# The last layer's loop in a four-layer transformer: another order of work, queries in SBUF, mixing in smaller steps

## The chip, the cores and the metric

The kernel runs on one core of a Trainium2 chip. The metric is the device time of one execution in microseconds. The profile names the engines PE (TensorE, matrix products, with PEld for loading its weights), DVE (VectorE), ACT (ScalarE), POOL (GpSimd) and SP (SyncE, which issues DMAs).

## What is computed

The reference runs four transformer layers on an input of 16×256×128. Each layer has an attention and a second block, each behind a layer norm with a shift and a scale from a small conditioning vector, and each added to the input with a gate. Only the last layer matters here. Its attention runs over the first axis, of length 16, separately for each of the 256 columns, causally, with 16 heads of 8 numbers. Its second block is a channel mixing with the row before:

```
scores = einsum("bhqd,bhkd->bhqk", q, k) / sqrt(8)      # q, k index the axis of 16, b the 256 columns
attn = softmax(where(causal, scores, -inf))
x = x + ga * (attn @ v @ W_out + b_out)
h = layernorm(x) * (1 + cb) + sb
xr, xk = mu * h + (1 - mu) * h_prev                     # h_prev: the column before
x = x + gb * sigmoid(xr @ W_r.T) * (relu(xk @ W_k.T) ** 2 @ W_v.T)
```

## The kernel before

The data x lie in SBUF as 128 channels by 16 units of 256 columns; a unit u is one position of the attention's axis. A query of unit u needs the keys of units 0 to u, so the work of a unit grows with u. Since each column has its own tiny attention, the scores are no matrix product over columns. Instead, for unit u:

- `queries`: PE makes the query, 128×256, in PSUM (tile q in the pool ps_q).
- `scores`: DVE multiplies the query, plus its bias, with the keys of up to 8 units at once (tile qk). Above 8 keys the unit has two parts, c=0 and c=1.
- `heads`: PE sums over the 8 channels of a head (16 small products a part) into the tile S.
- `exps`: DVE takes the maximum (top) and subtracts it (E), ACT takes the exponential.
- `weights`: DVE sums over the keys and inverts (tot), POOL multiplies E by that.
- `spread`: PE spreads the weights back over the channels, half a part at a time, into one of two large PSUM tiles (ps_big).
- `weighted`: DVE multiplies them with the values (tile pv); after the second half POOL adds the keys up in a tree until one or two are left.
- `projected`: PE multiplies what is left with the output weights (tile A). `added`: ACT scales it (tile t) and POOL adds it to x.

The loop of `layer3` (L2301) runs over u from 0 to 18. In iteration u it does scores and heads of unit u, exps and weights of w=u-1, spread and weighted of z=u-2, projected and added of a=u-3. Beside that run generators, the sides: `keys3` makes keys and values of two later units, `mixing3` does the second block of two finished units (of one unit for the last two). Each `tick()` lets every side do its next step. Both begin with the normalisation `normed3`: mean by a product on PE, difference on DVE (ln_xc), square on ACT (ln_sq), mean on PE, logarithm and exponential on ACT, product on POOL. `mixing3` goes on with `shifted` (ACT, tile h3f), two mixed products of four matmuls on PE, a sigmoid made from absolute value, relu, exponential and logarithm on ACT (tiles h and r, a sum on POOL), relu and square for the other (kr), a product with W_v on PE, the gating on DVE (r), the sum on POOL and the output DMA on SP.

Inside the loop `strict` and `strict_all` are set, and `keep_in_program_order` then fixes the order on each engine as the program issues it. An engine that waits therefore holds up all that the program issued after it on that engine. PSUM has eight banks: four in ps_big, one for ps_q, three for `bank()`, which serves S, A and all steps of the sides. Most operations are recorded on one line, L225 (the class that keeps the order) or L271 (`mm`), so the profile is read by the names of tiles.

Of the kernel before, what the change touches and what calls it, by code (L numbers as in the profile page):

```python
# [23 lines left out]
P = 128  # L24
# [186 lines left out]
def bc(ap, shape):  # L211
    return ap.to_broadcast(shape)
# [20 lines left out]
class _Kernel:  # L233
# [1982 lines left out]
        m = self.mods[3]  # L2216
        self.act.activation(dst, src, AF.Identity, bias=m[:, 3 * half, b : b + 1], scale=m[:, 3 * half + 1, b : b + 1])

    def normed3(self, src, out):

        n = src.shape[-1]
        ps = self.bank()[:, :n]
        self.mm(ps, self.c("mean"), src)
        yield
        xc = self.ln.tile([P, BLK], F32, tag="ln_xc", name="ln_xc")[:, :n]
        self.dve.tensor_sub(xc, src, ps)
        sq = self.ln.tile([P, BLK], F32, tag="ln_sq", name="ln_sq")[:, :n]
        self.act.activation(sq, xc, AF.Square)
        yield
        ps = self.bank()[:, :n]  # L2230
        self.mm(ps, self.c("mean"), sq)
        yield
        self.act.activation(sq, ps, AF.Ln, bias=self.eps5)
        self.act.activation(sq, sq, AF.Exp, scale=-0.5)
        self.gps.tensor_mul(xc, xc, sq)
        out.append(xc)
        yield

    def keys3(self, blk):

        out = []
        yield from self.normed3(self.x[:, blk * BLK : (blk + 1) * BLK], out)
        h = self.h3[blk] = self.l3.tile([P, BLK], F32, tag="h3", name="h3", bufs=3)
        for i in range(2):
            self.shifted(h[:, i * T : (i + 1) * T], out[0][:, i * T : (i + 1) * T], 2 * blk + i, 0)
        yield
        for n, (dst, k) in enumerate(((self.k3, "a3_bk"), (self.v3, "a3_bv"))):
            ps = self.bank()
            self.mm(ps, self.w3[:, (n + 1) * P : (n + 2) * P], h)
            yield  # L2250
            self.act.activation(dst[:, 2 * blk : 2 * blk + 2, :].rearrange("p b t -> p (b t)"), ps, AF.Identity, bias=self.v(k))

    def mixing3(self, b0, nb):

        two, W = self.two3, nb * T
        x = self.x[:, b0 * T : (b0 + nb) * T]
        if nb == 2:
            yield
            yield
        out = []  # L2260
        yield from self.normed3(x, out)

        h = two.tile([P, 2, T + 1], F32, tag="h3f", name="h3f")
        self.gps.memset(h[:, :, 0:1], 0.0)
        for i in range(nb):
            self.shifted(h[:, i, 1:], out[0][:, i * T : (i + 1) * T], b0 + i, 1)
        yield

        def mixed(n):
            ps = self.bank()[:, :W]  # L2270
            o = ps.rearrange("p (b t) -> p b t", t=T)
            self.mm(o, self.mix[2 * n], h[:, :nb, 1:], start=True, stop=False)
            self.mm(o, self.mix[2 * n + 1], h[:, :nb, :T], start=False, stop=True)
            return ps

        ps = mixed(0)
        yield

        r = two.tile([P, BLK], F32, tag="r3", name="r3")[:, :W]
        l = self.h1[:, :W]  # L2280
        self.act.activation(l, ps, AF.Abs)
        self.act.activation(r, ps, AF.Relu, scale=-1.0)
        self.act.activation(l, l, AF.Exp, scale=-1.0)
        self.act.activation(l, l, AF.Ln, bias=self.one)
        self.gps.tensor_add(r, r, l)
        ps = mixed(1)
        yield
        k = two.tile([P, BLK], F32, tag="kr3", name="kr3")[:, :W]
        self.act.activation(k, ps, AF.Relu)
        self.act.activation(k, k, AF.Square)  # L2290
        self.act.activation(r, r, AF.Exp, scale=-1.0)
        ps = self.bank()[:, :W]
        self.mm(ps, self.wv3, k)
        yield
        for i in range(nb):
            c = slice(i * T, (i + 1) * T)
            self.dve.scalar_tensor_tensor(r[:, c], ps[:, c], self.mods[3][:, 5, b0 + i : b0 + i + 1], r[:, c], ALU.mult, ALU.mult)
        self.gps.tensor_add(x, x, r)
        self.nc.sync.dma_start(out=self.out[:, b0 * T : (b0 + nb) * T], in_=x)

    def layer3(self):  # L2301
        self.tables()
        m = self.mods[3]
        with ExitStack() as ctx:
            self.ps_big = self.pool("ps_big", 2, PSUM, ctx=ctx)
            self.ps_q = self.pool("ps_q", 1, PSUM, ctx=ctx)
            self.ps_one = self.pool("ps_three", 3, PSUM, ctx=ctx)
            two = self.two3 = self.ln = self.pool("a3_two", 2, ctx=ctx)
            C = 32
            U = [{} for _ in range(B)]  # L2310
            sides = []

            def tick():
                for g in list(sides):
# [7 lines left out]
                return [(0, n)] if n <= 8 else [(0, (n + 1) // 2), ((n + 1) // 2, n)]  # L2322

            def queries(u):
                q = U[u]["q"] = self.ps_q.tile([P, T], F32, tag="q", name="ps_q")
                self.mm(q, self.w3[:, :P], self.h3[u // 2][:, u % 2 * T : (u % 2 + 1) * T])

            def scores(u, c):
                d = U[u]
                k0, k1 = parts(u)[c]  # L2330
                n = k1 - k0
                p = d["p", c] = self.wide.tile([P, 8, T], F32, tag="qT", name="qk")
                self.dve.scalar_tensor_tensor(
                    p[:, :n], bc(d["q"].unsqueeze(1), [P, n, T]), self.v("a3_bq"), self.k3[:, k0:k1, :], ALU.add, ALU.mult
                )

            def heads(u, c):
                d = U[u]
# [39 lines left out]
            def weighted(u, c, half):  # L2378
                d = U[u]
                k0, k1 = parts(u)[c]  # L2380
                n = k1 - k0
                if half == 0:
                    d["w", c] = (self.w if c else self.wide).tile([P, 8, T], F32, tag="wqkv" if c else "kT", name="pv")
                p = d["w", c]
                o = p[:, :n, half * P : (half + 1) * P].rearrange("p k (g c) -> p g k c", c=C)
                v = self.v3[:, k0:k1, half * P : (half + 1) * P].rearrange("p k (g c) -> p g k c", c=C)
                self.dve.tensor_mul(o, d.pop(("X", c, half))[:, :, :n], v)
                if half == 1:

                    add = (self.dve if u == B - 1 and c == 1 else self.gps).tensor_add  # L2390
                    while n > 2:
                        h = n // 2
                        add(p[:, :h], p[:, :h], p[:, n - h : n])
                        n -= h
                    d["n", c] = n
# [6 lines left out]
                    self.mm(d["A"], self.wo3, p, start=k == 0, stop=k == len(P_) - 1)  # L2402

            def added(u):
                t = two.tile([P, T], F32, tag="t3", name="t3")
                self.act.activation(t, U[u]["A"], AF.Identity, bias=self.go3[:, u : u + 1], scale=m[:, 2, u : u + 1])
                xb = self.x[:, u * T : (u + 1) * T]
                self.gps.tensor_add(xb, xb, t)
                U[u] = None
                if u >= B - 2:  # L2410
                    sides.append(self.mixing3(u, 1))
                elif u % 2:
                    sides.append(self.mixing3(u - 1, 2))

            self.strict = self.strict_all = True
# [2 lines left out]
            for u in range(B + 3):  # L2420
                w, z, a = u - 1, u - 2, u - 3
                b = u // 2 + 3
                if u % 2 == 0 and b < NBLK:
                    made[b] = self.keys3(b)
                    sides.append(made[b])
                if u == B + 2:
                    projected(a)
                    added(a)
                    break
                on_u, on_w, on_z, on_a = (0 <= i < B for i in (u, w, z, a))  # L2430
                two_u, two_z = on_u and u >= 8, on_z and z >= 8
                if on_z:
                    spread(z, 0, 0)
                    spread(z, 0, 1)
                if on_w:
                    exps(w)
                if on_u:
                    scores(u, 0)
                tick()
                if on_z:  # L2440
                    weighted(z, 0, 0)
                if two_z:
                    spread(z, 1, 0)
                if on_u:
                    heads(u, 0)
                if on_w:
                    weights(w)
                if on_a:
                    projected(a)
                if on_z:  # L2450
                    weighted(z, 0, 1)
                if two_z:
                    spread(z, 1, 1)
                tick()
                if two_u:
                    scores(u, 1)
                if two_z:
                    weighted(z, 1, 0)
                    tick()
                if two_u:  # L2460
                    heads(u, 1)
                if two_z:
                    weighted(z, 1, 1)
                if on_a:
                    added(a)
                tick()
                if u + 1 < B:
                    g = made.pop((u + 1) // 2, None)
                    if g in sides:
# [1 line left out]
                            pass  # L2471
                        sides.remove(g)
                    queries(u + 1)
                tick()
            while sides:
                tick()
            self.strict = self.strict_all = False
# [29 lines left out]
```

## Time and profile before

| what | value |
|---|---|
| timed runs | 2811.62, 2819.05, 2821.82 us, median 2819.05 |
| profiled execution | 2796.98 us, span from first to last instruction 2795.3 us |
| busy over the span | PE 2533.1 us (91%), DVE 1859.2 (67%), ACT 1588.3 (57%), POOL 1255.8 (45%) |
| mean granted clock of PE | 0.969 |
| the last layer | from 2574 us to the end of the span |

In the views below, a group's row gives line, engine, operation and out<-in with the shapes; a wait's row gives who waited for whom, the total in us, how often, and the longest. "Idle before" names the instruction that ended an engine's wait. The profiled execution is one execution and is 22 us shorter than the median of the timed runs; sums of rows are made against its own time.

### The profile page before, as it was taken

The page shows a single profiled execution, that of the slowest core. Times are in us where ns is not written, and L with a number is a line of the kernel's source. Part 1 is how long each engine was busy: PE and PEld are TensorE (multiplying, and loading weights), DVE is VectorE, ACT ScalarE, POOL GpSimd, SP SyncE. Part 2 cuts the span into 40 slices and gives each one's busy share as a digit, 9 for nine tenths or more (in the row PEclk, how much of TensorE's full clock was granted, in tenths as well). Part 3 has the DMA queues.
Part 4 walks back from the last instruction along what each step waited for, and adds up shares of the span by engine and source line. Part 5 has one row for each costly group of instructions (what it writes and reads, how often), then busy time and mean ns, then how long its engine had stood idle before and what let it go on. Part 6 is the DMA issues. An engine that isn't in the chain of part 4 may idle for free.

```text
span 2795.3 us, 50159 instructions
## 1 busy us (share of the span) xinstructions
PE 2533.1 (91%) x17702; PEld 1674.2 (60%) x17702; DVE 1859.2 (67%) x4448; ACT 1588.3 (57%) x4166; POOL 1255.8 (45%) x1105
## 2 busy tenths in 40 slices
PE   7999999989799999999999888899978998999886
PEld 4566565655588677777767545557745565444443
DVE  6777777787654466666666778783367885654664
ACT  4666666666544555666666366675535655542523
POOL 5776786886413553344434300233566442000555
PEclk9999999999999999999999899998989999999988
DMA  9230000000177300000000122326733331221000
GB/s 334 36 42 1 7 10 1 11 27 5 36 213 216 98 16 1 3 1 1 1 31 5 43 93 78 108 67 192 222 91 107 99 93 48 80 82 58 8 8 16
DMA packets 119434, 181.23 MB, mean 65 GB/s; under 512 B 18112, under 2 KB 81152, under 8 KB 116880
## 3 DMA queue, kind: packets, MB, share of 16 engines
q1 hardware_dynamic: 97504, 148.64, 17.9%
q0 software_dynamic: 8432, 17.31, 2.1%
q10 hardware_dynamic: 13248, 12.06, 1.3%
q8 instruction: 142, 2.33, 0.3%
q14 instruction: 108, 0.88, 0.1%
HBM read 120.51 MB, written 60.58 MB: 65 GB/s over the span
## 4 chain that ended last, share of the span: by engine, by line
PE 51%; DVE 22%; ACT 13%; POOL 5%; issue 5%; DMA 2%; SPq 1%; DVEq 0%; ACTq 0%; POOLq 0%
PE ps_one L271 23%; PE ps_big L271 8%; ACT E L225 7%; PE ps_one L274 6%; PE ps_out L271 5%; PE ps_hid L271 4%; DVE m L225 4%; POOL E L225 3%; PE ps_max L271 3%; DVE PT L225 2%; DVE r_t L225 2%; DVE sm_neg L225 1%; ACT r_sq L225 1%; PE ps_exp L271 1%; SPq L1431 1%
## 5 line engine op out<-in xcount | busy, mean ns | idle before, releaser
L225 POOL TENSOR_TENSOR E<-E,sm_inv 128x1024 f32<-128x1024 f32 (+1 forms) x246 | 412.8, 1688 | 502.6 <-DVE sm_inv L225 464.8
L225 ACT ACTIVATE E<-E,sm_neg 128x256 f32<-128x256 f32 x512 | 252.8, 495 | 198.3 <-DVE sm_neg L1216 198.3
L225 ACT ACTIVATE E<-ps_exp 128x1024 f32<-128x1024 f32 x246 | 225.9, 918 | 153.5 <-PE ps_exp L271 142.1
L225 DVE TENSOR_REDUCE m<-ps_max 128x4 f32<-128x1024 f32 x242 | 263.7, 1090 | 68.4 <-PE ps_max L271 67.6
L274 PEld LDWEIGHTS ps_one<-w_cst,E 128*128 128x128 f32 x1792 | 207.0, 144 | 150.1 <-POOL E L225 90.1
L225 ACT ACTIVATE E<-ps_big,sm_neg 128x128 f32<-128x128 f32 (+1 forms) x512 | 208.5, 421 | 145.7 <-DVE sm_neg L225 119.8
L274 PE MATMUL ps_one<-w_cst,E 128*128 128x128 f32 x1792 | 244.0, 281 | 49.8 <-POOL E L225 31.0
L225 POOL DMA_INDIRECT rows<-list_rows,l_i x128 | 127.8, 999 | 337.1 <-DVE a L225 152.8
L225 DVE COPY PT<-ps_one 128x512 f32<-128x512 f32 x320 | 203.1, 679 | 72.7 <-PE ps_one L274 72.3
L271 PE MATMUL ps_big<-kT,qT 64*128 64x256 f32 (+1 forms) x2048 | 243.7, 368 | 0.0
L271 PE MATMUL ps_one<-PT,v 128*64 128x256 f32 (+1 forms) x2048 | 225.5, 362 | 4.9 <-ACT v L225 3.2
L225 POOL DMA_INDIRECT list_rows<-done,origin x128 | 122.6, 958 | 169.5 <-ACT s L1104 54.3
L271 PEld LDWEIGHTS ps_big<-kT,qT 64*128 64x128 f32 x2048 | 173.7, 190 | 24.0 <-issue 10.4
L1216 DVE CUSTOM_DVE_ANT_0 E<-ps_big,bias 128x256 f32<-128x256 f32 x512 | 181.7, 420 | 8.9 <-PE ps_big L271 6.9
L271 PEld LDWEIGHTS ps_one<-PT,v 128*64 128x64 f32 x2048 | 132.1, 138 | 83.9 <-DVE sm_neg L1216 17.2
L225 POOL TENSOR_TENSOR r_r<-r_r,r_t 128x512 f32<-128x512 f32 x128 | 163.9, 1281 | 25.1 <-DVE r_t L225 22.0
L271 PE MATMUL ps_max<-q,q 60*128 60x256 f32 (+3 forms) x1008 | 125.3, 325 | 49.7 <-DVE m L225 34.7
L225 DVE TENSOR_TENSOR r_r<-ps_rope,a_cw 128x512 f32<-128x512 f32 x128 | 88.2, 689 | 120.2 <-ACT r_sq L225 112.4
L271 PE MATMUL ps_rope<-w_a_qkv,hb 128*128 128x512 f32 x256 | 141.8, 639 | 20.8 <-DVE sm_inv L225 12.6
L225 POOL TENSOR_TENSOR ln_xc<-ln_xc,ln_sq 128x512 f32<-128x512 f32 (+1 forms) x41 | 51.1, 1246 | 230.6 <-ACT ln_sq L225 230.4
L225 POOL TENSOR_SCALAR_AFFINE_SELECT E<-E 128x512 f32<-128x512 f32 x128 | 84.5, 660 | 147.4 <-ACT E L225 147.2
L271 PEld LDWEIGHTS ps_max<-q,q 60*128 60x128 f32 (+1 forms) x1008 | 79.6, 193 | 113.5 <-DVE m L225 75.8
(353 smaller groups left out, 5793.4 us busy)
## 6 DMA issues: line engine op xcount, KB each, us to landing
q<-parts SPq DMA_DIRECT2D x256, 128.0 KB
rows<-zeros SPq DMA_DIRECT2D x8, 2048.0 KB
share<-comb_rows SPq DMA_DIRECT2D x128, 128.0 KB
parts<-parts SPq DMA_DIRECT2D x14, 1024.0 KB
list_w<-in_f_W SPq DMA_DIRECT2D x46, 257.0 KB
done<-l_o ACTq DMA_DIRECT2D x92, 128.0 KB
f_W<-in_f_W SPq DMA_DIRECT2D x27, 386.0 KB
f_room<-in_f_W SPq DMA_DIRECT2D x19, 386.0 KB
```

The source lines that it names most:

```text
L225: ins = f(*args, **kw)
L271: self.ordered(self.nc.tensor.matmul(out, lhsT, rhs, start=start, stop=stop, **kw))
L274: self.ordered(self.nc.tensor.transpose(out, in_, self.c("ident")))
L1216: nc.vector.tensor_tensor_reduce(e[:, i], S[:, i], bias[g][:, i, off : off + T], 1.0, BIG, ALU.add, ALU.min, neg[:, i : i + 1])
L1431: self.last_moved = self.tc.keep_in_program_order(self.nc.sync.dma_start(out=out, in_=in_)).ins
```

## The change

It reorders the iteration and what is needed for that:

- `queries` puts the query into a bank of `bank()`, and ACT copies it with its bias to SBUF (tile q3). `scores` becomes a plain product of two SBUF tensors. The pool ps_q is gone, and `bank()` has two banks in place of three; two new ones (ps_side) serve the sides.
- Both halves of a part are spread one after the other, and weighted one after the other. The first part of a unit is spread at the end of the iteration before.
- The tile pv of a unit's second part alternates between two places (it had one).
- An iteration has three ticks (it had four, or five with two parts); two more come for u of 16 and above.
- `mixing3` of a pair takes eleven steps with pauses between them, the relu branch first. `side_held` lets only one side at a time keep a bank over a pause.
- For the last two units `mixing3` is "quick": fewer pauses, and some steps of ACT and POOL go to DVE. `added` of these units is one DVE instruction; ACT adds their output bias to x beforehand.

The loop's new body, and the changed helpers (cut):

```diff
             def queries(u):
-                q = U[u]["q"] = self.ps_q.tile([P, T], F32, tag="q", name="ps_q")
-                self.mm(q, self.w3[:, :P], self.h3[u // 2][:, u % 2 * T : (u % 2 + 1) * T])
+                ps = self.bank()[:, :T]
+                self.mm(ps, self.w3[:, :P], self.h3[u // 2][:, u % 2 * T : (u % 2 + 1) * T])
+                q = U[u]["q"] = two.tile([P, T], F32, tag="q3", name="q3")
+                self.act.activation(q, ps, AF.Identity, bias=self.v("a3_bq"))
...
-                self.dve.scalar_tensor_tensor(
-                    p[:, :n], bc(d["q"].unsqueeze(1), [P, n, T]), self.v("a3_bq"), self.k3[:, k0:k1, :], ALU.add, ALU.mult
-                )
+                self.dve.tensor_mul(p[:, :n], bc(d["q"].unsqueeze(1), [P, n, T]), self.k3[:, k0:k1, :])
...
-                    d["w", c] = (self.w if c else self.wide).tile([P, 8, T], F32, tag="wqkv" if c else "kT", name="pv")
+                    pool, tag = (self.wide, "kT") if c == 0 else (self.w, "wqkv") if u % 2 else (two, "pv1")
+                    d["w", c] = pool.tile([P, 8, T], F32, tag=tag, name="pv", bufs=1 if c else 2)
...
                 if on_z:
-                    spread(z, 0, 0)
-                    spread(z, 0, 1)
+                    weighted(z, 0, 0)
+                    weighted(z, 0, 1)
                 if on_w:
                     exps(w)
                 if on_u:
                     scores(u, 0)
-                tick()
-                if on_z:
-                    weighted(z, 0, 0)
                 if two_z:
                     spread(z, 1, 0)
+                    spread(z, 1, 1)
+                tick()
+                if on_a:
+                    projected(a)
                 if on_u:
                     heads(u, 0)
                 if on_w:
                     weights(w)
                 if on_a:
-                    projected(a)
-                if on_z:
-                    weighted(z, 0, 1)
+                    added(a)
+                tick()
                 if two_z:
-                    spread(z, 1, 1)
-                tick()
+                    weighted(z, 1, 0)
+                    weighted(z, 1, 1)
                 if two_u:
                     scores(u, 1)
-                if two_z:
-                    weighted(z, 1, 0)
-                    tick()
-                if two_u:
-                    heads(u, 1)
-                if two_z:
-                    weighted(z, 1, 1)
-                if on_a:
-                    added(a)
                 tick()
+                if on_w:
+                    spread(w, 0, 0)
+                    spread(w, 0, 1)
                 if u + 1 < B:
...
                     queries(u + 1)
-                tick()
+                if two_u:
+                    heads(u, 1)
+                if u == B - 1:
+                    for i in (B - 2, B - 1):
+                        xb = self.x[:, i * T : (i + 1) * T]
+                        self.act.activation(xb, xb, AF.Identity, bias=self.go3[:, i : i + 1])
+                if u >= B:
+                    tick()
+                    tick()
```

The end of `mixing3` shows the steps; each `yield` is a pause until the next tick, and `quick` skips most of them:

```diff
+        ps = mixed(1)
+        if quick:
+            self.dve.tensor_scalar(k, ps, 0.0, None, ALU.max)
+            self.dve.tensor_mul(k, k, k)
+        else:
+            self.act.activation(k, ps, AF.Relu)
+            self.act.activation(k, k, AF.Square)
+        yield
...
+        ps = bank()[:, :W]
+        self.side_held = not quick
+        self.mm(ps, self.wv3, k)
         self.act.activation(r, r, AF.Exp, scale=-1.0)
-        ps = self.bank()[:, :W]
-        self.mm(ps, self.wv3, k)
-        yield
+        if not quick:
+            yield
         for i in range(nb):
             c = slice(i * T, (i + 1) * T)
             self.dve.scalar_tensor_tensor(r[:, c], ps[:, c], self.mods[3][:, 5, b0 + i : b0 + i + 1], r[:, c], ALU.mult, ALU.mult)
-        self.gps.tensor_add(x, x, r)
+        self.side_held = False
+        if not quick:
+            yield
+        (self.dve if quick else self.gps).tensor_add(x, x, r)
```

## The prediction

> **What bounds the kernel now.** The edit touches only the last layer, so I first cut the profile by time. The table of windows gives that layer's loop (2574 to 2771 us) and its tail:
>
> ```profile
> core 0: us, PE busy (x) PEld busy (x) DVE busy (x) ACT busy (x) POOL busy (x), PEclk, DMA share, GB/s
> 2574.00:2771.00 197.00, 155.92 (x1020) 79.48 (x1020) 122.23 (x162) 79.67 (x142) 104.85 (x101) 0.91 0.02 9
> 2771.00:2795.30 24.30, 12.10 (x40) 7.13 (x40) 2.67 (x7) 13.53 (x32) 7.56 (x11) 0.89 0.06 23
> ```
>
> No engine fills the loop: DVE works 122.2 of 197.0 us, so it is idle for 74.8 us, and DMA does next to nothing. I then asked the waits, over 2574 to 2796 us, what DVE waited for:
>
> ```profile
> DVE r L225 <- PE ps_one L271: 29.2, 7, 6.6
> DVE qk L225 <- PE ps_q L271: 27.8, 11, 5.4
> DVE pv L225 <- PE ps_one L271: 17.8, 6, 5.9
> ACT h3f L225 <- POOL h3f L225: 14.9, 7, 3.9
> ```
>
> The first three are DVE queued in order behind the mixing's last product (r; 16.9 of its 29.2 us lie in the loop, 12.3 in the tail), the query product, and the output product that frees the one buffer of the second part (pv). The fourth shows how it starts: ACT waits for POOL, PE waits for ACT, DVE for PE. The timeline shows the price on PE and then on DVE (start, length, engine, operation, in brackets the idle time before):
>
> ```profile
> 2669.86 0.84 PE L271 MATMUL ps_big<-E,w_cst 32*128 32x160 f32 x8 [2.30 <-DVE pv L225]
> 2670.63 1.51 PE L271 MATMUL ps_one<-qk,w_cst 128*32 128x192 f32 x16
> ...
> 2681.84 3.78 PE L271 MATMUL ps_one<-h3f,mix 128*128 128x512 f32 x4 [2.78 <-ACT h3f L225]
> 2691.86 1.56 DVE L225 TENSOR_TENSOR pv<-ps_big,v 128x640 f32<-128x640 f32 x2 [5.90 <-PE ps_one L271]
> 2696.99 0.88 DVE L225 SCALAR_TENSOR_TENSOR r<-ps_one,mod,r 128x256 f32<-128x256 f32 x2 [3.57 <-PE ps_one L271]
> ```
>
> After 2.78 us of idleness the four mixing products take 3.78 us; at 2692.42 the same four take 1.99. So a PE that has idled also runs slower (granted clock 0.50 from 2684 to 2688 us), and DVE behind it idles 5.90 and 3.57 us.
>
> **Iterations.** I date iteration u by the subtraction that opens its softmax (E<-ps_one,top). Iterations 4 to 7 take 33.5 us (2593.63 to 2627.15), 8 to 11 take 51.1 (to 2678.22), 12 to 15 take 64.9 (to 2743.13), 16 and 17 take 28.0 (to 2771.1), and 20 lie before.
>
> **The change, part by part.**
>
> *DVE's order.* Both halves of a part are spread before they are weighted, the query is made a whole weighting and softmax ahead of its use, and no mixing step is put next to its successor. That aims at the 27.8, 16.9 and 17.8 us above. The second buffer for pv takes away the last outright. DVE's own work at u=14, from the rows: four weightings 2×1.07+2×0.93=4.0, softmax of 14 keys 0.63+0.62+0.92+0.35=2.5, scores 2.35+2.08=4.4, half a pair's normalising and gating (0.67+0.88)/2=0.8; in all 11.7 us. The same sum gives 35.4 us for u=8 to 11, 45.5 for 12 to 15, 16 for 16 and 17.
>
> *Queries to SBUF.* ACT copies 16 queries (0.55 us each, the price of t<-ps_one). The wait is ACT's for the query product; behind it on ACT is the next softmax's exponential, which isn't due until DVE has done two weightings and the subtraction (3.2 us at u=14). From u=4 on that covers it; for u below 4, about 0.3 us each, 1 us in all. Scores then is a product of two SBUF tensors. No row has it at 2048 elements; two of 1024 (1.22 each, pv<-pv) make 2.3 to 2.4 us, against 2.35 now. Alone it is worth 0 to 0.06 us ×24, at most 1.5, and I count 0.
>
> *What that product may cost.* A DVE instruction with two SBUF tensors stretches where POOL works; one with a PSUM tensor doesn't. The nearest pair, then one stretch and its POOL neighbours:
>
> ```profile
> L225 DVE SCALAR_TENSOR_TENSOR acc<-list_rows,list_room,ps_one x32: 318/342/348, 874.4 to 1113.0; 128x128 f32<-128x128 f32 x32
> L225 DVE SCALAR_TENSOR_TENSOR acc<-list_rows,list_room,acc x32: 337/346/975, 875.5 to 1118.5; 128x128 f32<-128x128 f32 x32
> ```
> ```profile
> 709.08 3.47 DVE L225 TENSOR_TENSOR E<-E,sm_inv 128x512 f32<-128x512 f32 x1
> 709.72 1.05 POOL L225 TENSOR_TENSOR r_r<-r_r,r_ss 128x512 f32<-128x512 f32 x1
> 710.72 1.27 POOL L225 TENSOR_TENSOR r_r<-r_r,r_t 128x512 f32<-128x512 f32 x1
> ```
>
> The first holds 318 to 348 ns in all 32; the second reaches 975. At 709.08 a DVE product of 0.69 us lasts 3.47 and ends when POOL's run of instructions pauses. At 589.71 (0.96 us where 0.34 is usual) it got in between two POOL instructions. So until now scores and POOL overlapped, and from now on they take turns: an iteration can't be shorter than POOL's work plus scores. POOL at u=14: trees 3.16+2.62, weights 1.13, x 0.73, half of a pair's three products (3.9/2=1.95), 9.6 us; with scores 14.0, more than DVE's 11.7. The sums by this rule: u=8 to 11, 10.0+10.9+10.4+11.4=42.7; u=12 to 15, 12.3+13.2+14.0+14.9=54.4; u=16 and 17 (no scores) 10.8+8.3=19.1.
>
> [...]
>
> [...] A wait of one POOL instruction's rest is in the exclusive sum already. For POOL standing idle when weights(w) waits for scores and the sum, I add half a POOL instruction, 0.7 us, to each of 14 iterations: 10 us.
>
> *u=4 to 7.* Here a chain binds: weightings, softmax, scores, sum and reciprocal, POOL's product, spread. From the rows at u=4: 0.8+0.75+1.3+0.7+0.6+0.75 and five hand-overs of 0.1, 5.4 us; with the exclusive sum at u=7 (6.6+2.35=9.0), 5.5+6+7+9=27.5 against 33.5.
>
> *Mixing and keys.* The counts stay; a pair takes 12 calls at three places (four iterations), so two pairs run at once. The added bank holds cost a call now and then, no engine time. PSUM stays at eight banks: 4 for spread, 2 for bank(), 2 at the side. Three uses an iteration of two banks may cost PE 0 to 0.5 us each, beside DVE's work; I take 0. The output DMAs stay nine issues of 0.33 us on SP, behind nothing else.
>
> *PE.* Its in-order queue at u=14: spreads 4.1, heads 1.9, output product 2.0, query 0.6, half a pair's seven products 3.6, 12.2 us at full clock, under 14.0. The new wait is spread(w,0) for POOL's weights, and behind it stand the query and the second heads. The row after 2.30 us of idleness (heads 1.51 where 0.86 is usual, output product 2.90 where 1.99 is) prices a lapse at 1.6 us. Eight such gaps would be 13 us of PE time, mostly under POOL's turn; 0 in the sum, 13 in rival C. [...] The rows decide: 2.30 us slowed PE here, and 2.06 us before 2733.74 did too (heads 1.32 for 1.07).
>
> *Tail.* Now 19.2 us from the last output product (2771.13) to the last output DMA, then 5.0 to the span's end. The new chain at 256 columns from the rows: 1.13+0.48+0.70+0.41+0.40+0.70+0.45+0.42+0.42+0.59+1.0+0.9+0.38+0.42+0.51+0.42+0.42+0.48+0.42=10.7, hand-overs 1.8, steps of the pair and of unit 14 between them 3: 15.5, a gain of 4. The two bias additions on ACT (0.4 each) run beside.
>
> **Sum.** New loop from u=4: 27.5+42.7+54.4+19.1+10=153.7 against 177.5, a gain of 24; tail 4; early loss 1: 27 us. The profiled execution took 2796.98 us (span 2795.3 and 1.7 around it), so it would take 2770. It lies 22 us under the median of the three timed runs, 2819.05; I take the gain off the median: 2792.
>
> **Rivals.**
> *A: no taking of turns matters, DVE is the bound.* For: many two-tensor products in the trace show no stretch. Against: POOL is busy here over half the time. Then DVE's sums plus 5% hold for the four stretches, 26+37+48+17=128 instead of 177.5, and the tail gains 4: 54 us, 2765.
> *B: the forecast*, turns as summed, with waits between none and 1.4 us an iteration (10 us either way) and 4 us either way for the chain before u=8 and the PSUM banks: a gain of 13 to 41, 2778 to 2806.
> *C: PE's order keeps the iteration.* heads(u,0) now stands behind the output product, which waits for POOL's trees; with lapses PE needs 12.2+1.6 and two waits of 1 us, about 16, what an iteration lasts now. Then only half of what u=4 to 7, 16 and 17 were to gain is left, 3+4, with the tail's 4 and the early loss of 1: 10 us, 2809.
> *D: scores starves behind POOL.* If POOL's queue is full (it is in the exclusive sum), scores waits for all of it, as at 709.08: a tree and a mixing product, 3.16+1.27=4.4 us, 16 times from u=8 to 15. DVE then needs 35.4+45.5+70=151 where those iterations take 116 now; less 15 gained in 16, 17 and the tail, and 4 lost before: 24 slower, 2843. It breaks even at about 3 us a wait. For: the 3.47 row. Against: 589.71 and the single stretches, where DVE got in after one instruction.
> *That the order isn't what it says* can hardly be: the loop keeps program order on every engine.
>
> **How the numbers follow.** B 0.50, A 0.20, C 0.18, D 0.12. The time is B's. The range leaves out D and the outer edge of A: 2760 to 2816. About 0.5%, 14 us, is what a measurement of this kernel can tell from no change. Faster: A, nine tenths of B and a little of C, 0.69; same: the rest of B and most of C, 0.18; slower: D and a little of C, 0.13.
>
> **What would show it.** Right: the layer's windows lose about 28 us; DVE's waits for ps_q and for pv's buffer vanish; qk lasts well over 2.35 us in many of its 24 instances, and POOL's products stretch beside it; granted clock near 1.0 in u=12 to 15. A: qk stays at its length and DVE is busy over 85%. C: idle time before heads on PE, released by POOL pv. D: qk of 5 us and more. The forecast is wrong if qk doesn't stretch, or if the layer's share doesn't shrink.

## The result: slower by half a per cent, and the profile after

The changed kernel takes 2833.96 us (median of five runs, 2826.53 to 2837.95) against 2819.05 before: a ratio of 1.0053 [1.0031, 1.0075]. Run once more on another chip it gave 1.0030 [1.0011, 1.0049]. That is 14.9 us more on the first chip and 8.8 on the second. The forecast was 2792.

The profiled execution before had its last layer begin at 2573.9 us. In the changed kernel it begins at 2595.1, and between 2580 and 2609 in every later run, although the instructions ahead of it are the same. So the spans are not compared here, but the layer alone: 221.4 us before, 229.7 after, 8.3 more. Dated as in the prediction (iteration u begins at the subtraction that opens its softmax, which is unit u-1's; the tail begins at the end of the last tree), its stages are, in us:

| stage | before | forecast | after | off by |
|---|---|---|---|---|
| u below 4 | 19.8 | 20.8 | 27.1 | 6.3 |
| 4 to 7 | 33.5 | 30.3 | 47.9 | 17.6 |
| 8 to 11 | 51.1 | 45.5 | 49.5 | 4.0 |
| 12 to 15 | 64.9 | 57.2 | 54.9 | -2.3 |
| 16, 17 | 27.9 | 20.5 | 24.2 | 3.7 |
| tail | 24.2 | 20.2 | 26.1 | 5.9 |
| layer | 221.4 | 194.5 | 229.7 | 35.2 |

(The forecast column holds the prediction's sums with 0.7 us added to each iteration from u=4 on.) From u=8 on the iterations came within 4 us of the forecast, stage by stage. Those of u=4 to 7, which were to gain 3 us, lost 14 against before, and those below 4 lost 7.

The table of windows of the changed kernel shows this stage by stage (u below 4, 4 to 7, 8 and 9, 10 and 11, 12 to 15, 16 and 17, tail):

```profile
core 0: us, PE busy (x) PEld busy (x) DVE busy (x) ACT busy (x) POOL busy (x), PEclk, DMA share, GB/s
2595.10:2622.19 27.09, 19.68 (x141) 9.59 (x142) 11.10 (x26) 11.29 (x22) 4.39 (x7) 0.81 0.00 1
2622.19:2670.06 47.87, 35.48 (x189) 16.68 (x187) 24.20 (x33) 21.80 (x40) 22.96 (x22) 0.86 0.00 1
2670.06:2695.98 25.92, 19.11 (x137) 9.09 (x138) 17.28 (x20) 11.86 (x22) 17.42 (x13) 0.87 0.03 11
2695.98:2719.53 23.55, 21.32 (x167) 11.72 (x166) 19.95 (x25) 12.76 (x24) 19.98 (x16) 0.99 0.03 12
2719.53:2774.48 54.95, 45.22 (x326) 25.01 (x326) 46.93 (x47) 20.59 (x37) 50.34 (x33) 0.93 0.03 11
2774.48:2798.73 24.25, 19.31 (x71) 10.16 (x68) 11.72 (x14) 9.37 (x16) 16.60 (x14) 0.71 0.03 11
2798.73:2824.80 26.07, 14.62 (x46) 8.15 (x44) 9.95 (x22) 11.11 (x23) 3.83 (x4) 0.89 0.09 31
```

In u=4 to 7 no engine is full (DVE works 24.2 of 47.9 us), and PE's granted clock is 0.86 where it was 1.00 before. The same stage of the kernel before:

```profile
2593.63:2627.15 33.52, 28.53 (x185) 14.04 (x186) 21.48 (x34) 19.58 (x37) 16.15 (x19) 1.00 0.02 7
```

The waits of DVE in the changed kernel's layer tell who is late:

```profile
DVE pv L225 <- PE ps_big L271: 50.8, 13, 11.2
DVE ln_xc L225 <- PE ps_side L271: 13.7, 4, 7.6
DVE qk L225 <- ACT q L225: 5.6, 3, 3.3
```

The three waits that the change aimed at (27.8, 16.9 and 17.8 us) are gone. The largest of the new ones is weighting's for the spread, 13 times, once for 11.2 us. The timeline of PE before that longest one shows why (start, length, operation, in brackets the idle time before):

```profile
2655.03 1.94 PE L271 MATMUL ps_one<-qk,w_cst 128*32 128x256 f32 x16 [3.60 <-DVE qk L225]
2656.89 3.78 PE L271 MATMUL ps_side<-h3f,mix 128*128 128x512 f32 x4
2660.47 1.36 PE L271 MATMUL ps_side<-ln_sq,w_cst 128*128 128x512 f32 x2
2664.10 1.66 PE L271 MATMUL ps_side<-h,w_a_qkv 128*128 128x512 f32 x2 [2.27 <-ACT h L225]
2665.69 1.89 PE L271 MATMUL ps_big<-E,w_cst 32*128 32x224 f32 x16
```

Between heads (ps_one<-qk) and spread (ps_big<-E) stand the products of the sides: mixing, a mean, and the keys, the last one waiting 2.27 us for ACT. In u=7 there is no second part, so the second and third tick follow each other with nothing between. PE reaches the spread at 2665.69, 8.7 us after heads end. POOL's weights were not what it waited for: their product had ended at 2657.41. DVE stands still meanwhile:

```profile
2656.08 0.35 DVE L225 RECIPROCAL tot<-tot 128x32 f32<-128x32 f32 x1
2667.60 2.09 DVE L225 TENSOR_TENSOR pv<-ps_big,v 128x896 f32<-128x896 f32 x2 [11.17 <-PE ps_big L271]
```

The turns with POOL came too. Here is the scores' row (shortest, median and longest ns), and then before's:

```profile
L225 DVE TENSOR_TENSOR qk<-q,k x24: 426/2292/3321, 2596.6 to 2768.2; 128x1280 f32<-128x1280 f32 x5, 128x1536 f32<-128x1536 f32 x5, 128x1792 f32<-128x1792 f32 x5, 128x2048 f32<-128x2048 f32 x4
```
```profile
L225 DVE SCALAR_TENSOR_TENSOR qk<-ps_q,w_vecs,k x24: 484/1810/2351, 2574.7 to 2736.4; 128x1280 f32<-128x1280 f32 x5, 128x1536 f32<-128x1536 f32 x5, 128x1792 f32<-128x1792 f32 x5, 128x2048 f32<-128x2048 f32 x4
```

In the layer qk takes 52.3 us of DVE where it took 41.4, and 11 of its 24 instances last longer than 2.35 us. POOL's trees (pv) take 72.8 us where they took 52.2, its products with E 16.5 for 12.2.

### The profile page after: what moved, and what is told of

Read it like the earlier page. It is cut to its first block, busy times and chain, and to the rows that moved or that the text cites. A ratio compares the mean times of both kernels' runs of the same rounds, so it can differ in the third digit from the quotient of the medians.

```text
span 2824.8 us, 50165 instructions
## 1 busy us (share of the span) xinstructions
PE 2547.4 (90%) x17702; PEld 1678.7 (59%) x17702; DVE 1871.9 (66%) x4462; ACT 1594.3 (56%) x4176; POOL 1278.7 (45%) x1097
## 4 chain that ended last, share of the span: by engine, by line
PE 50%; DVE 23%; ACT 13%; POOL 6%; issue 5%; DMA 2%; SPq 1%; another core or an unknown queue 0%; DVEq 0%; ACTq 0%; POOLq 0%
PE ps_one L271 20%; PE ps_big L271 8%; ACT E L225 7%; PE ps_one L274 6%; PE ps_out L271 4%; DVE m L225 4%; PE ps_hid L271 4%; POOL E L225 4%; PE ps_max L271 3%; DVE PT L225 3%; DVE r_t L225 2%; PE ps_side L271 2%; DVE sm_neg L225 1%; PE ps_exp L271 1%; ACT r_sq L225 1%
## 5 line engine op out<-in xcount | busy, mean ns | idle before, releaser
L1216 DVE CUSTOM_DVE_ANT_0 E<-ps_big,bias 128x256 f32<-128x256 f32 x512 | 181.8, 421 | 12.2 <-PE ps_big L271 6.3
L225 POOL TENSOR_TENSOR ln_xc<-ln_xc,ln_sq 128x512 f32<-128x512 f32 x39 | 53.1, 1364 | 224.3 <-ACT ln_sq L225 224.1
```

The source lines that it names most:

```text
L225: ins = f(*args, **kw)
L1216: nc.vector.tensor_tensor_reduce(e[:, i], S[:, i], bias[g][:, i, off : off + T], 1.0, BIG, ALU.add, ALU.min, neg[:, i : i + 1])
```

## The experiments

Theory 1: PE's in-order queue, with the sides' products ahead of spread, sets the early iterations. Theory 2: the turns of the two-tensor scores with POOL cost the time. Theory 3: ACT's copy of the query is late; the text for e2 gave it no more than the 5.6 us that DVE waits for the copy. No time below is as much as 1% from the kernel before's; a run is called faster or slower where its interval leaves out 1. All runs, with the layer's stages in us and the ratio to the kernel before on the same chip:

| run | <4 | 4-7 | 8,9 | 10,11 | 12-15 | 16,17 | tail | layer | ratio |
|---|---|---|---|---|---|---|---|---|---|
| before | 19.8 | 33.5 | 23.0 | 28.1 | 64.9 | 27.9 | 24.2 | 221.4 | 1 |
| ctrl | 27.4 | 47.9 | 25.9 | 23.6 | 54.9 | 22.7 | 27.2 | 229.5 | 1.0030 [1.0011, 1.0049] |
| e1 | 25.4 | 36.8 | 36.3 | 24.3 | 57.1 | 24.1 | 26.0 | 230.1 | 1.0044 [1.0023, 1.0064] |
| e2 | 28.2 | 47.2 | 24.7 | 23.7 | 54.2 | 23.0 | 29.0 | 230.0 | 1.0024 [1.0000, 1.0048] |
| e3 | 21.2 | 30.6 | 32.2 | 25.3 | 55.1 | 23.0 | 29.0 | 216.4 | 0.9976 [0.9955, 0.9997] |
| e4 | 22.2 | 36.0 | 27.9 | 31.8 | 66.6 | 30.9 | 25.0 | 240.4 | 1.0061 [1.0042, 1.0081] |
| e5 | 25.4 | 36.8 | 30.0 | 23.5 | 56.8 | 22.7 | 24.6 | 219.8 | 0.9992 [0.9979, 1.0005] |
| e6 | 21.2 | 30.6 | 30.6 | 23.7 | 55.0 | 22.9 | 29.0 | 213.0 | 0.9979 [0.9957, 1.0002] |
| e7 | 20.7 | 29.5 | 28.7 | 23.6 | 54.9 | 23.0 | 22.8 | 203.3 | 0.9952 [0.9933, 0.9970] |
| e8 | 24.4 | 37.5 | 25.0 | 31.4 | 64.7 | 28.0 | 24.2 | 235.2 | 1.0059 [1.0032, 1.0085] |
| e9 | 25.5 | 35.3 | 29.0 | 23.6 | 56.3 | 22.7 | 24.2 | 216.6 | 0.9994 [0.9978, 1.0010] |
| e10 | 21.2 | 32.0 | 26.6 | 21.9 | 46.0 | 23.0 | 24.3 | 195.0 | 0.9906 [0.9875, 0.9936] |
| e11 | 20.6 | 29.5 | 28.8 | 24.1 | 54.6 | 23.0 | 22.7 | 203.3 | 0.9963 [0.9941, 0.9985] |
| e12 | 25.3 | 34.7 | 28.9 | 23.5 | 55.0 | 23.5 | 24.3 | 215.2 | 0.9993 [0.9970, 1.0016] |
| e13 | 25.5 | 36.8 | 27.3 | 21.8 | 54.4 | 22.8 | 24.2 | 212.7 | 0.9954 [0.9935, 0.9973] |

A stage of one profile is good to about 2.5 us: e7 and e10 run the same instructions in u=4 to 7 and take 29.5 and 32.0. The chips differ (before's median is 2820, 2822, 2803 and 2826 us in the four groups), so times are compared by ratio.

**ctrl** is the changed kernel again.

> The changed kernel once more, beside the kernel before on one chip. If the 21 us that its profile shows ahead of the last layer (before 1982 us) come from the chip and not from the change, since the instructions there are the same, the start of the last layer lies again anywhere within 2574 to 2600 us, while the layer itself again takes 8 us (6 to 11) more than the 221.4 us of before. Ratio to before 1.003 to 1.008.

**e1: the spread ahead of the ticks.** For u below 10, spread(w,0) and the next query are issued before the second tick:

```
                if on_a:
                    added(a)
+               if not two_z:
+                   handed(u, w, on_w)     # spread(w, 0, 0), spread(w, 0, 1), queries(u + 1)
                tick()
                ...
                tick()
-               (the same two spreads and queries(u + 1))
+               if two_z:
+                   handed(u, w, on_w)
```

> The changed kernel, but in iterations whose unit z has one part (u up to 9) the spreads of w and the query of u+1 are issued ahead of the second and third tick instead of behind them. Theory 1 (the side products that stand on PE between heads(u,0) and the spreads are the loss of the early iterations): DVE's wait for ps_big falls from 50.8 us to under 25, iterations 0 to 9 (from the layer's start to the softmax of u=10, 100.9 us in the changed kernel) shrink by 15 to 25 us, total about 2814 us (ratio to before 0.995 to 1.001). Theory 2 (the turns that POOL and the product of two SBUF tensors take are the loss): the early iterations shrink by less than 5 us, total about 2830. Theory 3 (the query's copy on ACT is late): no change beyond 3 us, as the copy stays.

u=4 to 7 became 11.1 us shorter, as theory 1 has it, but u=8 and 9 took 10.4 back, so that iterations 0 to 9 shrank by 2.3 us and not by its 15 to 25, and the time did not move. In these two, all that is issued on PE after the spread now stood behind its wait for POOL's weights (2.0 and 2.2 us): both ticks' products and, last of all, heads(u,1), which the next softmax needs. One wait of DVE for such a side product lasts 8.83 us:

```profile
2675.74 0.69 DVE L225 TENSOR_TENSOR ln_xc<-x,ps_side 128x512 f32<-128x512 f32 x1 [8.83 <-PE ps_side L271]
```

**e2: the query stays in PSUM**, and scores adds the bias as before the change; S keeps one bank:

```
-               ps = self.bank()[:, :T]
-               ...
-               q = U[u]["q"] = two.tile([P, T], F32, tag="q3", name="q3")
-               self.act.activation(q, ps, AF.Identity, bias=self.v("a3_bq"))
+               q = U[u]["q"] = qa[:, :T]       # half a PSUM bank; A takes the other half
+               ...
-               self.dve.tensor_mul(p[:, :n], ...)
+               self.dve.scalar_tensor_tensor(p[:, :n], ..., ALU.add, ALU.mult)
```

> The changed kernel, but the query stays in PSUM (half of a bank, the output product's sum in the other half, one bank left for the scores) and scores reads it there with its bias, as before; there is no copy on ACT. Theory 2: qk falls from 52.3 us to 41 to 42, POOL's trees from 72.8 to 52 to 54 us, and the layer from 229.7 to 210 to 216 us, total about 2818. Theory 1: qk and POOL's trees fall just as much, but the early iterations (0 to 9) by less than 6 us, since PE's queue there is unchanged; the later ones by 5 to 10; total 2820 to 2828. Theory 3: the gain is all in the first iterations and no more than the 5.6 us of waits for the copy.

qk went back to 41.3 us, POOL's pv to 52.3 and E to 12.2, some 36 us of engine time, and the layer stayed at 230.0; DVE's wait for the spread grew from 50.8 to 56.7 us. e2's one bank for S may hide 2 to 3 us of gain: its tail is 29.0 us. Theory 2 falls as the cause of the slowdown. So does one of my readings: that the 54.9 us of u=12 to 15 bear out the exclusive sum of 54.4. Without any turns they are 54.2.

**e3: both edits.** This kernel computes units 8 and 9 wrong: their second part's scores use the query of the unit after, and wait for it. So its time stands for the order only; e6 below has both edits with the right scores.

> Both edits of the two runs before. Theory 1 with theory 2 as a smaller part: the gains add, 20 plus 8 us, layer near 202 us, total about 2806 us (ratio to before 0.993 to 0.998). If turns cost nothing once PE's queue is in order, it is the same as the first of the two alone; if PE's queue costs nothing, the same as the second alone.

Alone neither edit gained anything; together they gain 13.7 us of the layer over e1. With PE's queue out of the way, the copied query seems to cost; e5 and e6 show it with right scores (219.8 and 213.0, though e6 loses 4.4 us in the tail).

**e4: the copy alone, in the old order** (ACT copies the query from ps_q to SBUF, scores is a product of two SBUF tensors).

> The kernel before, with one edit: ACT copies the query to SBUF, so scores is a product of two SBUF tensors; order and buffers stay the old ones. Turn-taking, as a fact: qk goes from 41.4 to about 50 us of DVE time in the layer and POOL's pv from 52.2 to about 70, as the changed kernel and its run with the query in PSUM showed in the new order. Theory 1 (PE's order sets the new kernel's early iterations; the turns cost only where nothing else binds): in the old order DVE waits for PE's query product, so part of the longer scores takes the place of idle time: the layer goes from 221.4 to 222-230, the time to 2820-2829. Theory 2 (the turns are the cost of the change): the layer lengthens by the whole of it, 20 us and more, 2840.

The layer took 19 us more, theory 2's number. But this edit holds two things, the copy and the product, which **e8** takes apart: ACT copies the query to the other half of its PSUM bank.

```
-               q = U[u]["q"] = self.ps_q.tile([P, T], F32, tag="q", name="ps_q")
-               self.mm(q, ...)
+               ps = self.ps_q.tile([P, 2 * T], F32, tag="q", name="ps_q")
+               self.mm(ps[:, :T], ...)
+               q = U[u]["q"] = ps[:, T:]
+               self.act.activation(q, ps[:, :T], AF.Identity, bias=self.v("a3_bq"))
```

> The kernel before, with ACT copying the query (bias added) from one half of its PSUM bank to the other, so scores is the same product with one operand in PSUM: the copy and its place in the order are those of the run with the copy in SBUF (layer 240.4, time +20.8), without a product of two SBUF tensors. Turns as that run's price: qk back to about 41 us, POOL's pv to 52, and the layer at 225-230 (what is left is ACT's step ahead of scores: DVE's waits for the query grew from 27.8 to 36.0 there, 8 us), the time +5 to +9. Copy as the price (ACT's place in the chain): qk falls too, but the layer stays at 237-241, the time +18 to +21.

qk and pv are back at 39.9 and 52.2 us, and the layer is still 13.8 us longer than before's, between the two theories; the ratio is the same as e4's within its interval. DVE's wait at qk grew from 27.8 to 37.0 us. So most of the price is ACT's copy, not the turns: what I had put to theory 2 after e4 was wrong.

**e5, e6, e7: the order mended step by step.** e5 is e1 with the early spread for u below 8 alone; e6 adds e2's query in PSUM; e7 adds, in iteration 17, `projected(15)` and `added(15)` right behind weighted(15,1,·). (The last unit is 15; the texts on e7 and e9 call it 17.)

> The changed kernel with spread(w,0) and the next query moved ahead of the second and third tick for u below 8 alone; units 8 and 9 keep the changed order. Theory 1: u below 4 and 4 to 7 gain what they gained before (2 and 11 us), 8 and 9 stay at 26 us, nothing later moves: layer 217, the time about 13 us under the changed kernel's 2829, 2816, level with the kernel before. Rival (side work costs what it costs, and only moves to wherever there is no second part yet): 8 and 9 or 10 and 11 take the 10 us back again, layer 228-230, 2829.

> As the run before (spread first for u below 8), with the query left in PSUM. Theory 1 with turns that cost where PE no longer binds: u below 4 21, u=4 to 7 31, 8 and 9 25, 10 and 11 24, 12 to 15 54.5, 16 and 17 23, tail 29: layer 208, the time 2807, faster than the kernel before by 12. Rival (side work only moves): 8 and 9 stay at 32 and the layer at 216, 2814.

> As the run before, and the last output product (unit 17) is issued right after its tree, ahead of the mixing products that stood before it on PE's queue, and unit 17's mixing starts at once. Theory 1 (side products ahead on PE's queue cost the tail too: in the changed kernel the last tree ended at 2798.7 and its product began at 2804.9): the tail goes from 29 to about 23, the time 2801. Rival (the chains of the last pair and of unit 14 on ACT set the tail): the tail keeps its 29, 2807.

e5 is level with before, 10 us of layer better than the change; u=8 and 9 took some 4 us back, less than the rival had it. e6 lies between its two theories (213.0; 8 and 9 at 30.6). e7 is faster than before; its tail fell from 29.0 to 22.8. That cured what e6's edit, with one bank for S, had cost there: in e9, with two banks, the same edit moved the tail from e5's 24.6 to 24.2 only.

**e9 and e12: what the copy costs in the mended order.** e9 is e7 with the changed kernel's query in SBUF; e12 is e7 with ACT adding the bias in place in PSUM.

> The last run's mended order (spread first below u=8, unit 17's output product first) with the changed kernel's query in SBUF and its two banks for scores and products; against the run with the query in PSUM (2807.7, layer 203.3, of which tail 22.8) it shows what the copied query costs once PE's queue no longer stands in front. Turns (and copy) costing on the path where PE doesn't bind: u below 4 +4, u=4 to 7 +6, the rest 0 to +2 a stage, tail -2 to -4 (second bank): layer 211-214, time 2814-2818. If they were free: layer 200-203, time 2804.

> The mended order with the query in PSUM (layer 203.3; third tick where the changed kernel has it), and ACT adds the bias to the query in place in PSUM, so scores waits for ACT as in the changed kernel, but has one operand in PSUM. ACT's step as the price: u below 4 +4, u=4 to 7 +5, layer 212-216, time 8 to 12 us above that order's (ratio to before 0.998-0.9995). Turns as the price: layer 203-206, ratio 0.995-0.996.

e12 lost 11.9 us of e7's 203.3 and e9 13.3, most of it below u=8 (4.6 and 5.2 of e12's, 4.8 and 5.8 of e9's). The copy is the price there; the 1.4 us between e12 and e9, which has the turns too, are within what one profile is good to. The rows of waits up to u=7 show the way, e12 first, then e7:

```profile
ACT ps_qa L225 <- PE ps_qa L271: 19.2, 8, 3.8
DVE tot L225 <- ACT E L225: 9.8, 4, 3.0
```
```profile
DVE tot L225 <- ACT E L225: 4.6, 3, 2.5
```

ACT stops at the copy until PE has made the query, and PE makes it only behind spread(w,0); behind the copy on ACT stand the sides' steps and the next exponential, for which DVE then waits 5.2 us longer. Its other waits up to u=7 grew by 4 us: for the copy itself, for the sides' products and for the spread.

**e11: one pv buffer** for the second part in e7.

> The mended order with the query in PSUM (2807.7), and one buffer for the second part's pv again. The prediction took its second buffer as worth the 17.8 us that DVE waited in the old order. If so here: u=10 to 17 lose 10 us and more, time 2818, with DVE pv waits released by the output product. If the new order alone took that wait away (the output product now stands ahead of weighted(z,1) by half an iteration): time unchanged, 2807-2810.

The layer is 203.3 again. DVE waits for the output product at pv for 5.1 us in all, and the layer is no longer for it. So it is the order that made the 17.8 us harmless, not the second buffer.

**e10 and e13: the third tick last.** For u=8 to 15 the third tick moves from before spread(w,0) to the end of the iteration. e10 does it to e7, e13 to e9:

```
-               tick()
+               if not two_u:
+                   tick()
                ... spread(w, 0, ·), queries(u + 1)
                if two_u:
                    heads(u, 1)
+                   tick()
```

> The mended order with the query in PSUM (2807.7, layer 203.3), and from u=8 on the third tick moved from before spread(w,0) to the end of the iteration, behind the second heads. Theory 1 (side products between heads and spread stand in the loop that goes DVE, PE, DVE; the chain of waits of u=12 to 15 holds 2.0 to 4.5 us of them in an iteration, in two ticks): 8 and 9 lose 4, 10 to 17 lose about 1 each: layer 191-196, time 2796-2800. Rival (the side products only fill PE's wait for POOL's weights, which comes last): 10 to 17 stay, 8 and 9 lose at most 2, time 2806-2808, and PE shows waits ahead of spread released by POOL E.

> The mended order with the third tick last from u=8 on (layer 195.0, u=12 to 15 46.0 with the query in PSUM), here with the changed kernel's query copied to SBUF and its two banks. If the forecast's exclusive sum is a bound (POOL's work plus scores can't overlap): u=12 to 15 take 54 to 57, 10 and 11 24 or more, layer 213-216, ratio to before 0.998-1.000. If turns don't bind (rival A): 12 to 15 take 46 to 49, layer 204-208 (u below 8 keeps the copy's 10), ratio 0.994-0.996.

The reason for e10 is e7's chain of waits at u=14 (start, length, what):

```profile
2724.97 2.27 DVE qk L225
...
2727.28 1.99 PE ps_qa L271 x8
2729.28 1.00 PE ps_one L271 x16
2730.28 4.49 PE ps_side L271 x10
2734.77 1.07 PE ps_big L271 x16
2735.84 2.09 DVE pv L225 x2
2737.93 0.58 DVE top L225
...
2738.60 0.66 DVE E L225
2739.26 2.27 DVE qk L225
```

It is a loop of DVE and PE by turns, 14.3 us from qk to qk, and 4.5 of it are side products. Over u=12 to 15 the chain holds 12.1 us of them in e7 and 7.5 in e10. Much of the rest of the gain goes with the clock, granted 0.91 in e7's stage and 1.00 in e10's: two of e7's output products in the chain (ps_qa, 8 products) take 3.45 and 3.78 us, in e10 none takes over 1.99. u=12 to 15 fell from 54.9 to 46.0 us, and the whole is 0.9906 [0.9875, 0.9936] of the kernel before, 2777.99 against 2802.8 us on that chip: the best of all, and faster than both kernels. The windows of u=12 to 15, e10 and then e13:

```profile
2683.19:2729.17 45.98, 39.99 (x332) 21.52 (x326) 43.53 (x46) 19.19 (x35) 36.18 (x33) 1.00 0.04 13
```
```profile
2719.98:2774.36 54.38, 42.25 (x312) 22.48 (x308) 46.78 (x46) 18.70 (x34) 50.60 (x33) 0.87 0.03 11
```

In e10 DVE works 43.5 of 46.0 us: it is the bound at last. With the two-tensor scores (e13) POOL works 50.6 of 54.4 (36.2 in e10), its work stretched by the turns, and the stage takes the 54.4 us of the forecast's exclusive sum. e13 has the copy as well as the turns, and no run in this order has the copy alone. But its chain of waits in u=12 to 15 holds no copy: it runs from one POOL instruction to the next for some 38 of the 54 us, and PE waits there for POOL's weights, as the prediction had it:

```profile
PE ps_big L271 <- POOL E L225: 10.8, 3, 5.3
```

So the turns are a bound, 8.4 us here, but only once PE's queue is not. In the changed kernel both bounds are there (its chain runs over POOL for some 22 of the 55 us of this stage); that they are equally long, 54.4 and 54.2, is chance.

## Why the prediction was wrong, step by step

- *"u=4 to 7" failed*, 17.6 of the 35.2 us. Its chain ran from weighting to spread over DVE, ACT and POOL, and had none of the sides' products in it. On PE's in-order queue they stand within it: spread came 8.7 us after heads. Moving spread ahead of them took out 11.1 us (e1, e5); what is left, 36.8, is 5.2 to 5.8 us of the copy (e12, e9) and some 31. That this is close to the forecast's 30.3 is luck in part: that sum holds turns, and e7, without any, takes 29.5. Its rows at u=4 are also in part one iteration early (weightings 0.8 and scores 1.3, where iteration 4 has 0.55+0.49 and 1.55).
- *"Queries to SBUF" was mis-sized.* The early loss was put at 1 us, with the copy covered from u=4 on. It measured 4.6 below u=4 and 5.2 in 4 to 7 (e12 against e7), and 13.8 in the whole layer in the old order (e8). I looked at who waits behind the copy on ACT, but not at what the query product itself stood behind on PE.
- *"What that product may cost" held, and was off the path.* qk stretched by 11 us, POOL's pv by 21 and its E by 4; e2 gave all of it back and gained nothing. e13 shows the bound: 54.4 us where the exclusive sum had 54.4. The 2.8 us added in this stage for POOL standing idle were not seen there.
- *"DVE's order" held as far as it went.* The three waits vanished, and u=10 to 17 fell from 120.9 to 102.7 us (forecast for u=8 to 17: 20.7 us less; measured: 15.3). But "takes away the last outright" gave the second buffer a part that it has not (e11).
- *"PE" named the right place with the wrong cause.* It had the new wait at spread(w,0), for POOL's weights. But in the changed kernel's whole layer PE waits 0.5 us for these weights. What it came late from was the side products ahead of spread. Its sum of 12.2 us an iteration, under 14.0, said nothing of where in the iteration those products lie.
- *"Tail" failed* by 5.9 us. The chain of unit 15 was summed at 15.5 us from the last output product on, with 3 for the steps of others, and nothing ahead of it. But that product began 6.1 us after the tree's end at 2798.73, behind products of the last pair and of unit 14 on PE:

```profile
2797.98 3.51 PE L271 MATMUL ps_side<-h3f,mix 128*128 128x512 f32 x4 [3.16 <-ACT h3f L225]
...
2804.86 1.89 PE L271 MATMUL ps_one<-pv,w_a_o 128*128 128x256 f32 x8
```

From there to the last output DMA it took 16.7 us. Issuing the product first (e9 against e5) shortened the tail by 0.4 us only: DVE then waited 4.4 us for ACT, where the steps of units 14 and 15 stood behind the last pair's. No run with two banks brought the tail under 24.2, so how much of it could be won stays open. What kept u=8 to 11 and 16, 17 some 4 us each over the forecast was not taken apart either.
- *Rivals.* C, PE's order, came nearest in kind and in place (2809 forecast), but priced lapses and POOL's wait, and kept half of the early gain; the early iterations lost instead. D fell: the longest qk was 3.3 us, where it needed 5. A's 48 us for u=12 to 15 is close to e10's 46.0, in which its condition, no turns, holds.
- *The row at 709.08*, a wait over several POOL instructions, is what rival D was built on. It stays unexplained: in this layer's rows below, an engine's delay fits the rest of one instruction of the other. In e13 the longest qk ended 2.1 us after one POOL instruction had, and a POOL sum that usually takes 0.72 us ended 0.6 us after the DVE product beside it:

```profile
2752.71 2.41 DVE L225 TENSOR_TENSOR qk<-q,k 128x1792 f32<-128x1792 f32 x1
...
2758.37 3.35 DVE L225 TENSOR_TENSOR qk<-q,k 128x2048 f32<-128x2048 f32 x1
```
```profile
2753.20 2.53 POOL L225 TENSOR_TENSOR x<-x,t 128x256 f32<-128x256 f32 x1
...
2758.30 1.27 POOL L225 TENSOR_TENSOR x<-x,r 128x512 f32<-128x512 f32 x1
```

## What to carry to other kernels

On an in-order engine, background work has a price that its total doesn't show: list what stands between each critical instruction and the one before it, and put side work behind the instruction that the bottleneck waits for, not ahead of it. An edit can be worth nothing while another queue holds the iteration (e2), and 7 to 13 us once that is mended (e5 to e6, e9 to e7), so undo suspects in the mended order as well as in the given one. A copy that moves an operand to another engine's queue costs where that queue stops, not what the copy takes: e12's 16 copies are 7.1 us of ACT, and the layer is 11.9 us longer for them.

## What I had not expected of the hardware

PE did not run slower after every gap of 2.3 us and more, as the prediction had it. In e7, after 2.57 us of idleness, two products of 512 columns took 1.13 us (the two at 2652.78, with no gap before them, took 1.12); after 3.61 us four of 256 took 2.08, twice theirs (the four at 2651.14 took 1.03):

```profile
2649.32 1.13 PE L271 MATMUL ps_side<-h,w_a_qkv 128*128 128x512 f32 x2 [2.57 <-ACT h L225]
...
2651.14 1.03 PE L271 MATMUL ps_qa<-pv,w_a_o 128*128 128x256 f32 x4
...
2652.78 1.12 PE L271 MATMUL ps_side<-h,w_a_qkv 128*128 128x512 f32 x2
...
2663.44 2.08 PE L271 MATMUL ps_qa<-pv,w_a_o 128*128 128x256 f32 x4 [3.61 <-DVE qk L225]
```

In the kernel before, PE was slow behind two shorter gaps. Over the heads behind that of 2.30 us the granted clock was 0.50. Behind that of 2.06 us it was 0.57 over the output product, which took 3.38 us where 1.99 is usual (the clock stands third from the end of the windows' rows):

```profile
2670.63:2672.14 1.51, 1.51 (x19) 0.67 (x17) 1.51 (x4) 0.00 (x0) 1.12 (x2) 0.50 0.00 0
2735.95:2739.26 3.31, 3.31 (x13) 2.44 (x9) 2.78 (x2) 0.63 (x1) 3.23 (x3) 0.57 0.03 7
```
```profile
2733.74 1.03 PE L271 MATMUL ps_big<-E,w_cst 32*128 32x224 f32 x8 [2.06 <-DVE pv L225]
2734.69 1.32 PE L271 MATMUL ps_one<-qk,w_cst 128*32 128x256 f32 x16
2735.95 3.38 PE L271 MATMUL ps_one<-pv,w_a_o 128*128 128x256 f32 x8
```

So in these rows the length of the gap alone does not tell a slow stretch: 2.06 and 2.30 us were followed by one, 2.57 us was not. What else decides it is not shown here.
